# The order of eight running-maximum steps among the other VectorE work of a block, in the last stage of a four-layer kernel

## The chip, the cores and the metric

The kernel runs on one core of a Trainium2 chip. A core has five engines with instruction queues of their own: TensorE (PE in the profile, with its weight loads as PEld), VectorE (DVE), ScalarE (ACT), GpSimd (POOL) and SyncE (SP), which here only issues transfers. Each works through its queue in order, and they wait for one another, or for a transfer, through semaphores. The metric is the device time of one execution in microseconds, taken as the median of several runs.

## What is computed

The input `x` has 8 images of 32 channels, 256 rows and 256 columns, in fp32. Four layers follow one another, each of the form `x = x + conv(groupnorm(x))`: a spectral convolution, a 5 by 5 convolution, a recurrence over the columns, and a layer of directional maxima. The change lies in the last one:

```python
def _L3_conv_ref(x, W, b):
    x1 = cummax(x, axis=2)                 # down the rows
    x2 = cummax(x, axis=2, reverse=True)   # up the rows
    x3, x4 = ...                           # along the columns: from the left, from the right
    x_con = jnp.concatenate((x, x1, x2, x3, x4), axis=1)
    return jnp.einsum('bchw,oc->bohw', x_con, W[:, :, 0, 0]) + b[None, :, None, None]
x = x + _L3_conv_ref(_gn(x), L3_conv_W, L3_conv_b)
```

So each output is a mix, by a 160 to 32 matrix, of the normalised input and its running maxima in four directions.

## The kernel before

The stages run one after the other: `forward_and_mix` and `inverse_and_conv` (first two layers), `recurrence` (third layer), `maxima_and_mix` (last layer, from line 898, the only function that the change touches). The recurrence goes through the columns from left to right and leaves in device memory its output (`x3d`) and the maximum from the left (`fwd`), each as 32 blocks of 8 columns.

`maxima_and_mix` takes these blocks from the right end to the left, `bi` from 31 to 0, since the maximum from the right is carried from block to block. The rows of an image are folded by four: row 4q + a is element q (of Q = 64) of slot a (of A = 4). A tile has 128 partitions (four images of 32 channels), slots, two halves `b2` of the batch, 8 columns and 64 elements. The normalisation's scale is folded into the weights (`wsc`) and its shift into a bias (`bres`), so the maxima are taken of the values as they are.

Inside the loop the order on each engine is the order of the program text: `tc.manual_schedule(engines=None)` keeps the order written by hand. Semaphores for results and for buffers that come free are put in automatically. A block has these parts:

- **Loads** (`load`, line 965): SyncE issues the transfers of the next block, 2048 KB of `x3d` into `xt` and 2048 KB of `fwd` into `fw` (line 969). Both have two buffers.
- **VectorE, fifteen instructions.** Eight steps of the maximum from the right, column 7 down to column 0 (lines 989 to 994): each takes the maximum of the column and the result to its right, so each needs the one in front of it; the first needs column 0 of the block before (`after`). They write `rev` (tile `rv`, two buffers). Then the maxima over the rows: pairs of slots (line 1002, into `xt[:, A:A+2]`), all four slots (1003, into `top`), a scan over the 64 elements downwards into `dq` and one upwards into `uq` (1005, 1006), and three instructions that go back from folded to single rows, into `m` (1007, 1008, 1009). `m`, `dq`, `uq` and `top` have one buffer each.
- **TensorE, the mix** (`mix`, line 1019, and 1031 to 1036): for each half and each of the five terms, 16 products of 32 by 32 weights with 512 columns, all summed in PSUM, in four banks of a half. Two halves of two blocks take all eight banks. An fp32 product shows as two records, so a block has 320. Terms 0 (`x`), 3 (`fws`) and 4 (`rvs`, the maxima from the right) are mixed first for both halves; then come, half by half, 1 (`downs`) and 2 (`ups`), which need `m`, `dq` and `uq`.
- **ScalarE**: after a half's last term, four activations add the bias and move the four banks into `ot` (line 1039, three buffers), and ScalarE's queue issues its transfer to `out` (line 1040, 1024 KB).

```python
                for t, src in ((0, x), (3, fws), (4, rvs)):
                    for b2 in range(2):
                        mix(b2, t, src, first=t == 0)
                for b2 in range(2):
                    mix(b2, 1, downs)
                    mix(b2, 2, ups, last=True)
```

Of the kernel before, what the change touches and what calls it, by code (L numbers as in the profile page):

```python
# [11 lines left out]
ALU = mybir.AluOpType  # L12
# [11 lines left out]
A = 4  # L24
# [873 lines left out]
def maxima_and_mix(tc, k, d, x3d, fwd, mv3, mean1, out):  # L898


    nc = tc.nc
    WB = 8
    NB = W // WB
    with ExitStack() as ctx:
        one = ctx.enter_context(tc.tile_pool(name="cc", bufs=1))
        blk = ctx.enter_context(tc.tile_pool(name="cb", bufs=2))
        op = ctx.enter_context(tc.tile_pool(name="co", bufs=3))
        ps = ctx.enter_context(tc.tile_pool(name="cp", bufs=2, space=PSUM))

        w3 = one.tile([P, 5, C], F32, name="w3")  # L910
        b3 = one.tile([P, 1], F32, name="b3")
        nc.gpsimd.dma_start(out=w3.rearrange("p t o -> p (t o)"), in_=d["w3T"])
        nc.gpsimd.dma_start(out=b3, in_=d["b3"])


        sta, _ = finish_stats(tc, one, ps, k, mv3, B, k.pair, "c", "o1", 2)
        st = one.tile([P, 2, 2], F32, name="st3")
        for i in range(4):
            q = slice(32 * i, 32 * i + 32)
            nc.vector.tensor_copy(st[q], sta[q, i::4, :])  # L920
        shift = one.tile([P, 2], F32, name="shift3")
        nc.vector.scalar_tensor_tensor(shift, st[:, :, 0], -1.0, st[:, :, 1], ALU.mult, ALU.mult)
        wsc = one.tile([P, 2, 5, C], F32, name="wsc")
        for b2 in range(2):
            nc.vector.tensor_scalar_mul(wsc[:, b2], w3, st[:, b2, 1:2])

            nc.vector.tensor_tensor(wsc[:, b2, 0], wsc[:, b2, 0], k.ident32, ALU.add)


        wsum = one.tile([P, A, C], F32, name="wsum")  # L930
        nc.vector.tensor_tensor(wsum[:, 0], w3[:, 0], w3[:, 1], ALU.add)
        for t in range(2, 5):
            nc.vector.tensor_tensor(wsum[:, 0], wsum[:, 0], w3[:, t], ALU.add)
        for j in range(1, A):
            nc.vector.tensor_copy(wsum[:, j], wsum[:, 0])
        sel = one.tile([P, 2, 4], F32, name="sel")
        nc.vector.memset(sel, 0.0)
        for i in range(4):
            q = slice(32 * i, 32 * i + 32)
            nc.vector.tensor_copy(sel[q, :, i], shift[q])  # L940
        bp = ps.tile([P, 2, 4], F32, name="bp", tag="o0")
        nc.tensor.matmul(
            bp.rearrange("p b i -> p (b i)"),
            lhsT=wsum.rearrange("p j o -> p (j o)"),
            rhs=sel.rearrange("p b i -> p (b i)"),
            start=True,
            stop=True,
        )
        bres = one.tile([P, 2, 4], F32, name="bres")
        nc.vector.tensor_scalar_add(bres, bp, b3[:, 0:1])  # L950
        nc.vector.tensor_tensor(bres, bres, mean1.rearrange("p (b i) -> p b i", b=2), ALU.add)


        QP = Q + 2
        cuts = one.tile([P, 2, 2 * WB, QP], F32, name="cuts")
        nc.vector.memset(cuts, BIG)
        nc.vector.memset(cuts[:, 0, :, 0:1], -BIG)
        nc.vector.memset(cuts[:, 1, :, QP - 1 : QP], -BIG)
        cutf = cuts.rearrange("p s w q -> p s (w q)")
        top = one.tile([P, 2, WB, QP], F32, name="top")  # L960
        nc.vector.memset(top, -BIG)

        xs = {}

        def load(bi):

            for src, tag, n in ((x3d, "x3", A + 2), (fwd, "fw", A)):
                t = xs[bi, tag] = blk.tile([P, n, 2, WB, Q], F32, name=f"{tag}_{bi}", tag=tag)
                nc.sync.dma_start(out=t[:, 0:A].rearrange("p a b w q -> p (a b) (w q)"), in_=src[bi].rearrange("p a b n -> p (a b) n"))

        def flat(t):
            return t.rearrange("p s b w q -> p s (b w q)")

        def rows_of(t):
            return t.rearrange("p s b w q -> p s (b w) q")

        def twice(t):
            return t.rearrange("p b w q -> p (b w) q").unsqueeze(1).to_broadcast([P, 2, 2 * WB, Q])

        after = None  # L980
        with tc.manual_schedule(engines=None):
            load(NB - 1)
            for bi in range(NB - 1, -1, -1):
                if bi > 0:
                    load(bi - 1)
                xt, fw = xs.pop((bi, "x3")), xs.pop((bi, "fw"))
                rev = blk.tile([P, A, 2, WB, Q], F32, name=f"rv_{bi}", tag="rv")
                if after is not None:
                    nc.vector.tensor_tensor(rev[:, :, :, WB - 1, :], after, xt[:, 0:A, :, WB - 1, :], ALU.max)
                else:  # L990
                    nc.vector.tensor_copy(rev[:, :, :, WB - 1, :], xt[:, 0:A, :, WB - 1, :])
                for w in range(WB - 2, -1, -1):
                    nc.vector.tensor_tensor(rev[:, :, :, w, :], rev[:, :, :, w + 1, :], xt[:, 0:A, :, w, :], ALU.max)  # L993
                after = rev[:, :, :, 0, :]

                x = [xt[:, a] for a in range(A)]

                m = blk.tile([P, 6, 2, WB, Q], F32, name=f"m_{bi}", tag="m", bufs=1)
                dq = blk.tile([P, 2, WB, QP], F32, name=f"dq_{bi}", tag="dq", bufs=1)
                uq = blk.tile([P, 2, WB, QP], F32, name=f"uq_{bi}", tag="uq", bufs=1)  # L1000
                tt = nc.vector.tensor_tensor
                tt(flat(xt[:, A : A + 2]), flat(xt[:, 0:A:2]), flat(xt[:, 1:A:2]), ALU.max)  # L1002
                tt(top[:, :, :, 1 : 1 + Q], xt[:, A], xt[:, A + 1], ALU.max)
                df, uf, tf = (t.rearrange("p b w q -> p (b w q)") for t in (dq, uq, top))
                nc.vector.tensor_tensor_scan(df, cutf[:, 0], tf, -BIG, ALU.min, ALU.max)  # L1005
                nc.vector.tensor_tensor_scan(uf[:, ::-1], cutf[:, 1, ::-1], tf[:, ::-1], -BIG, ALU.min, ALU.max)
                tt(rows_of(m[:, 2:4]), twice(dq[:, :, :, 0:Q]), rows_of(xt[:, 0 : A + 1 : A]), ALU.max)  # L1007
                tt(rows_of(m[:, 0:2]), twice(uq[:, :, :, 2 : 2 + Q]), rows_of(xt[:, A - 1 : A + 2 : 2]), ALU.max)  # L1008
                tt(flat(m[:, 4:6]), flat(m[:, 1:4:2]), flat(xt[:, 1:3]), ALU.max)  # L1009
                downs = [m[:, 2], m[:, 3], m[:, 5], dq[:, :, :, 1 : 1 + Q]]  # L1010
                ups = [uq[:, :, :, 1 : 1 + Q], m[:, 4], m[:, 1], m[:, 0]]

                fws, rvs = [fw[:, a] for a in range(A)], [rev[:, a] for a in range(A)]
                pts = [
                    [ps.tile([P, 2 * H], F32, name=f"o_{bi}_{b2}_{i}", tag=f"o{i}") for i in range(4)] for b2 in range(2)
                ]


                def mix(b2, t, src, first=False, last=False):
                    for j in range(A):  # L1020
                        for i in range(4):
                            q = slice(32 * i, 32 * i + 32)
                            nc.tensor.matmul(  # L1023
                                pts[b2][i][32 * j : 32 * j + 32].rearrange("p (w q) -> p w q", q=Q),
                                lhsT=wsc[q, b2, t, :],
                                rhs=src[j][q, b2],
                                start=first,
                                stop=last,
                            )

                for t, src in ((0, x), (3, fws), (4, rvs)):
                    for b2 in range(2):
                        mix(b2, t, src, first=t == 0)
                for b2 in range(2):
                    mix(b2, 1, downs)
                    mix(b2, 2, ups, last=True)
                    ot = op.tile([P, 4, 2 * H], F32, name=f"ot_{bi}_{b2}", tag="ot")
                    for i in range(4):
                        nc.scalar.activation(ot[:, i], pts[b2][i], AF.Identity, bias=bres[:, b2, i : i + 1])  # L1039
                    nc.scalar.dma_start(out=out[bi, b2], in_=ot)  # L1040
# [140 lines left out]
```

## Time and profile before

| what | value |
|---|---|
| median of three runs | 3231.57 us (3227.11, 3231.57, 3237.39) |
| span of the profiled execution, first to last instruction | 3226.3 us |
| time of the profiled execution apart from its span | not given; the span is 0.8 us below the fastest of the three runs |
| busy over the span | PE 89%, DVE 81%, ACT 58%, POOL 27% |
| last stage, first load issued to the end of the span | 2545.7 to 3226.3 us, 680.6 us |
| DVE busy from 2600 to 3100 us, per 100 us | 97.9 to 98.1 us |
| PE busy in the same stretches | 75.9 to 78.6 us |
| moved by the transfers in the same stretches | 305 to 316 GB/s |

How to read what follows: rows of the profile name the line, engine, operation, output tile and input tiles, shapes (partitions times elements) and a count. In an answer in order of time the first number is the start in us from the span's start, the second the time from there to the end of the row; a bracket at its end gives the idle time of the engine before it and what ended it. Rows with the same line that stand in sequence are merged into one with a count. In the slices of the page each digit is a fortieth of the span, in tenths. In the table by stretches the columns are: the stretch, its length, the busy time of PE, PEld, DVE, ACT and POOL with instruction counts, the granted clock of TensorE as a share of full speed, the transfer engines' busy share, and GB/s.

### The profile page before, as it was taken

How to read it: one execution, taken by the hardware profiler on the slowest of the kernel's cores; microseconds unless marked ns; L12 is line 12 of the kernel's file. 1: busy time of each engine (PE TensorE's matmuls, PEld its weight loads, DVE VectorE, ACT ScalarE, POOL GpSimd, SP SyncE). 2: the span in 40 equal slices, each digit the busy share in tenths (PEclk: the TensorE clock that was granted, in tenths of full speed). 3: DMA queues.
4: the chain of work that ended last, by engine and by line, in shares of the span. 5: the costliest groups of instructions: out<-in, count | busy, mean ns of one | idle time of the engine just before them, and what ended most of it. 6: DMA issues, size and time to landing. Idle time of an engine off the chain costs nothing.

```text
span 3226.3 us, 112014 instructions
## 1 busy us (share of the span) xinstructions
PE 2866.3 (89%) x47802; PEld 1666.4 (52%) x47802; DVE 2614.3 (81%) x5188; ACT 1862.5 (58%) x4362; POOL 860.8 (27%) x1241
## 2 busy tenths in 40 slices
PE   7975799999999969999999999999999577777776
PEld 4655344444444446666666666666666233333332
DVE  5742577777767759999999999999999799999998
ACT  3422365565565657888888888888887222222222
POOL 0110011111111145555555555555555200000000
PEclk9985899999999989999999999999999788888998
DMA  9978577888777545665555555666554588878885
GB/s 385 387 288 193 129 187 193 196 194 195 186 182 197 138 110 153 159 159 151 146 148 147 147 146 151 157 159 159 155 143 121 188 306 305 308 311 314 313 308 217
DMA packets 527058, 655.75 MB, mean 203 GB/s; under 512 B 388825, under 2 KB 389737, under 8 KB 500829
## 3 DMA queue, kind: packets, MB, share of 16 engines
q1 hardware_dynamic: 483628, 494.33, 53.9%
q0 software_dynamic: 17200, 85.05, 8.1%
q10 hardware_dynamic: 25728, 69.21, 5.4%
q8 instruction: 374, 6.13, 0.8%
q14 instruction: 128, 1.04, 0.1%
HBM read 371.63 MB, written 272.63 MB: 200 GB/s over the span
## 4 chain that ended last, share of the span: by engine, by line
PE 54%; DVE 25%; DMA 8%; SPq 6%; issue 5%; ACT 2%; POOL 0%; DVEq 0%; ACTq 0%; POOLq 0%
PE r L742 13%; PE z L742 12%; PE ni L742 6%; PE nh L742 6%; DMA x2d<-x 6%; SPq L547 5%; DVE rv L993 5%; PE vp L490 4%; DVE x L527 3%; PE yp L131 3%; DVE dq L1005 2%; DVE m L1009 2%; DVE m L1007 2%; DVE x L1002 2%; DVE m L1008 2%
## 5 line engine op out<-in xcount | busy, mean ns | idle before, releaser
L750 PE MATMUL z<-hs,weights 64*64 64x256 f32 x4080 | 539.4, 382 | 0.0
L750 PE MATMUL r<-hs,weights 64*64 64x256 f32 x4080 | 525.2, 375 | 0.0
L750 PE MATMUL ni<-hs,weights 64*64 64x256 f32 x4080 | 524.9, 375 | 0.0
L832 POOL TENSOR_TENSOR xw<-xw,hs 128x256 f32<-128x256 f32 x496 | 339.5, 684 | 635.6 <-DVE hs L831 635.6
L527 DVE SCALAR_TENSOR_TENSOR x<-vp,r,x 64x512 f32<-64x512 f32 (+2 forms) x640 | 350.8, 563 | 164.6 <-PE vp L490 137.8
L1039 ACT ACTIVATE ot<-o,bres 128x512 f32<-128x512 f32 x256 | 155.4, 690 | 541.5 <-PE o L1023 533.9
L490 PE MATMUL vp<-x,c_conv 64*64 64x384 f32 (+2 forms) x4608 | 457.5, 514 | 0.2
L826 POOL TENSOR_TENSOR a<-zm,xn 128x256 f32<-128x256 f32 x510 | 372.7, 731 | 6.4 <-issue 6.2
L1023 PE MATMUL o<-m,wsc 32*32 32x512 f32 x3072 | 237.1, 830 | 152.9 <-DVE m L1009 106.3
L824 ACT ACTIVATE n<-n,bih 128x256 f32<-128x256 f32 x510 | 260.8, 511 | 184.4 <-DVE n L823 184.4
L490 PEld LDWEIGHTS vp<-x,c_conv 64*64 64x64 f32 x4608 | 238.3, 138 | 234.5 <-issue 128.5
L742 PE MATMUL z<-xn,weights 64*64 64x256 f32 x2040 | 305.3, 376 | 24.2 <-ACT xn L722 24.2
L742 PE MATMUL r<-hs,weights 64*64 64x256 f32 x2040 | 319.0, 389 | 4.4 <-DVE hs L831 3.4
L742 PE MATMUL r<-xn,weights 64*64 64x256 f32 x2040 | 305.6, 376 | 1.0 <-ACT rs L817 1.0
L742 PE MATMUL nh<-xn,weights 64*64 64x256 f32 x2040 | 305.7, 376 | 0.0
L742 PE MATMUL z<-hs,weights 64*64 64x256 f32 x2040 | 305.2, 376 | 0.0
L742 PE MATMUL ni<-hs,weights 64*64 64x256 f32 x2040 | 305.2, 375 | 0.0
L722 ACT ACTIVATE xn<-xw,shift,turned 128x256 f32<-128x256 f32 x496 | 291.9, 589 | 0.0
L750 PEld LDWEIGHTS ni<-hs,weights 64*64 64x64 f32 x4080 | 284.4, 133 | 0.3
L818 DVE SCALAR_TENSOR_TENSOR n<-nh,bhh,rs 128x256 f32<-128x256 f32 x510 | 246.3, 483 | 45.3 <-ACT rs L817 30.7
L750 PEld LDWEIGHTS r<-hs,weights 64*64 64x64 f32 x4080 | 281.1, 131 | 0.2
L817 ACT ACTIVATE rs<-r,brz 128x256 f32<-128x256 f32 x510 | 242.7, 476 | 50.8 <-PE r L750 30.3
(165 smaller groups left out, 6267.2 us busy)
## 6 DMA issues: line engine op xcount, KB each, us to landing
xb<-in_xl_dram POOLq DMA_DIRECT2D x96, 768.0 KB, 6.4
xa<-in_xt_dram SPq DMA_DIRECT2D x64, 1024.0 KB
x<-x3d SPq DMA_DIRECT2D x32, 2048.0 KB
fw<-fwd SPq DMA_DIRECT2D x32, 2048.0 KB
out_dram<-ot ACTq DMA_DIRECT2D x64, 1024.0 KB
xw<-x2d SPq DMA_DIRECT2D x31, 2048.0 KB
fwd<-fm SPq DMA_DIRECT2D x248, 256.0 KB
x3d<-xw SPq DMA_DIRECT2D x248, 256.0 KB
```

The costliest lines, as they stand in the source:

```text
L490: ins = nc.tensor.matmul(vps[bank][to], lhsT=k.conv[r, P : P + 64] if kind == 2 else k.conv[r, o], rhs=pair_of(u, ch, g, lo, hi, (2, 0)[i] ...
L527: nc.vector.scalar_tensor_tensor(x, src[o], r1[rows, g : g + 1], x, ALU.mult, ALU.add, accum_out=s1[rows, 0, n, ch, g : g + 1])
L547: (nc.gpsimd if 2 * u + ch == 2 * n - 1 and p % 2 else nc.sync).dma_start(out=x2d[b, a, c0 : c0 + CH, TS * t + lo : TS * t + hi].rearrange ...
L722: nc.scalar.activation(norms[bi][:, b, w], raws[bi][:, b, w], AF.Identity, bias=shift[:, b : b + 1], scale=sc[:, 1, b : b + 1])
L742: ins = nc.tensor.matmul(out[r], lhsT=weights[r, kind, gate, :], rhs=src[r], start=start, stop=stop)
L750: ins = nc.tensor.matmul(out[pairs[1 - i]], lhsT=weights[r, kind, gate, :], rhs=prev[r, :, q0 : q0 + Q], start=False, stop=stop,)
L817: rs = nc.scalar.activation(r, p["r"], AF.Sigmoid, bias=brz[:, 0:1])
L818: nc.vector.scalar_tensor_tensor(m, p["nh"], bhh[:, 2:3], r, ALU.add, ALU.mult)
L824: nc.scalar.activation(m, m, AF.Tanh, bias=bih[:, 2:3])
L826: product = nc.gpsimd.tensor_tensor(a, zm, cur, ALU.mult)
L832: nc.gpsimd.tensor_tensor(raw, raw, new, ALU.add)
L1023: nc.tensor.matmul(pts[b2][i][32 * j : 32 * j + 32].rearrange("p (w q) -> p w q", q=Q), lhsT=wsc[q, b2, t, :], rhs=src[j][q, b2], start=first,
```

## The change

The eight steps become a function `back(w)`, and its calls stand between the other VectorE instructions of the block: step 7 behind the pair maxima, then one step behind each following instruction, and steps 1 and 0 both behind the last. On TensorE the maxima from the right, term 4, go from third to last: `x`, `fws`, `downs` and `ups` are mixed for both halves, and then each half gets its `rvs` and is emptied. Number, operations and shapes of the instructions and the buffers stay as they are.

```diff
                 rev = blk.tile([P, A, 2, WB, Q], F32, name=f"rv_{bi}", tag="rv")
-                if after is not None:
-                    nc.vector.tensor_tensor(rev[:, :, :, WB - 1, :], after, xt[:, 0:A, :, WB - 1, :], ALU.max)
-                else:
-                    nc.vector.tensor_copy(rev[:, :, :, WB - 1, :], xt[:, 0:A, :, WB - 1, :])
-                for w in range(WB - 2, -1, -1):
-                    nc.vector.tensor_tensor(rev[:, :, :, w, :], rev[:, :, :, w + 1, :], xt[:, 0:A, :, w, :], ALU.max)
-                after = rev[:, :, :, 0, :]
...
+                def back(w):
+                    last = after if w == WB - 1 else rev[:, :, :, w + 1, :]
+                    if last is None:
+                        nc.vector.tensor_copy(rev[:, :, :, w, :], xt[:, 0:A, :, w, :])
+                    else:
+                        tt(rev[:, :, :, w, :], last, xt[:, 0:A, :, w, :], ALU.max)
+
                 tt(flat(xt[:, A : A + 2]), flat(xt[:, 0:A:2]), flat(xt[:, 1:A:2]), ALU.max)
+                back(7)
                 tt(top[:, :, :, 1 : 1 + Q], xt[:, A], xt[:, A + 1], ALU.max)
+                back(6)
                 nc.vector.tensor_tensor_scan(df, cutf[:, 0], tf, -BIG, ALU.min, ALU.max)
+                back(5)
                 nc.vector.tensor_tensor_scan(uf[:, ::-1], cutf[:, 1, ::-1], tf[:, ::-1], -BIG, ALU.min, ALU.max)
+                back(4)
                 tt(rows_of(m[:, 2:4]), twice(dq[:, :, :, 0:Q]), rows_of(xt[:, 0 : A + 1 : A]), ALU.max)
+                back(3)
                 tt(rows_of(m[:, 0:2]), twice(uq[:, :, :, 2 : 2 + Q]), rows_of(xt[:, A - 1 : A + 2 : 2]), ALU.max)
+                back(2)
                 tt(flat(m[:, 4:6]), flat(m[:, 1:4:2]), flat(xt[:, 1:3]), ALU.max)
+                back(1)
+                back(0)
+                after = rev[:, :, :, 0, :]
...
-                for t, src in ((0, x), (3, fws), (4, rvs)):
+                for t, src in ((0, x), (3, fws), (1, downs), (2, ups)):
                     for b2 in range(2):
                         mix(b2, t, src, first=t == 0)
                 for b2 in range(2):
-                    mix(b2, 1, downs)
-                    mix(b2, 2, ups, last=True)
+                    mix(b2, 4, rvs, last=True)
                     ot = op.tile([P, 4, 2 * H], F32, name=f"ot_{bi}_{b2}", tag="ot")
```

More of the change, by code (lines that the diff above doesn't have):

```diff
@@ L1001, in maxima_and_mix @@
                 tt = nc.vector.tensor_tensor
+                df, uf, tf = (t.rearrange("p b w q -> p (b w q)") for t in (dq, uq, top))
+                def back(w):
[4 more added lines that the diff above has]
+                        tt(rev[:, :, :, w, :], last, xt[:, 0:A, :, w, :], ALU.max)
                 tt(flat(xt[:, A : A + 2]), flat(xt[:, 0:A:2]), flat(xt[:, 1:A:2]), ALU.max)
+                back(7)
                 tt(top[:, :, :, 1 : 1 + Q], xt[:, A], xt[:, A + 1], ALU.max)
-                df, uf, tf = (t.rearrange("p b w q -> p (b w q)") for t in (dq, uq, top))
+                back(6)
                 nc.vector.tensor_tensor_scan(df, cutf[:, 0], tf, -BIG, ALU.min, ALU.max)
+                back(5)
                 nc.vector.tensor_tensor_scan(uf[:, ::-1], cutf[:, 1, ::-1], tf[:, ::-1], -BIG, ALU.min, ALU.max)
+                back(4)
                 tt(rows_of(m[:, 2:4]), twice(dq[:, :, :, 0:Q]), rows_of(xt[:, 0 : A + 1 : A]), ALU.max)
+                back(3)
                 tt(rows_of(m[:, 0:2]), twice(uq[:, :, :, 2 : 2 + Q]), rows_of(xt[:, A - 1 : A + 2 : 2]), ALU.max)
+                back(2)
                 tt(flat(m[:, 4:6]), flat(m[:, 1:4:2]), flat(xt[:, 1:3]), ALU.max)
+                back(1)
+                back(0)
+                after = rev[:, :, :, 0, :]
                 downs = [m[:, 2], m[:, 3], m[:, 5], dq[:, :, :, 1 : 1 + Q]]
```

## The prediction

> **What bounds the kernel now.** I read the page's slices first, to find the stage that the change touches, then VectorE's instructions in order of time for one block of that stage, then TensorE's and ScalarE's for the same block, then granted clocks by stretch, and last the end of the chain of waits.
>
> The slices (80.7 us each): the last stage is the last eight or nine digits.
>
> ```profile
> PE   7975799999999969999999999999999577777776
> DVE  5742577777767759999999999999999799999998
> ```
>
> From slice 32 on DVE is at 9 and PE at 7. In the stage VectorE is nearly always busy, TensorE is not. One block of it on VectorE (columns: start us, us, engine, line, operation, tiles, count):
>
> ```profile
> 2859.94 2.29 DVE L1009 TENSOR_TENSOR m<-m,x 128x2048 f32<-128x2048 f32 x1
> 2862.15 0.68 DVE L989 TENSOR_TENSOR rv<-rv,x 128x512 f32<-128x512 f32 x1
> 2862.87 5.05 DVE L993 TENSOR_TENSOR rv<-rv,x 128x512 f32<-128x512 f32 x7
> 2867.84 2.28 DVE L1002 TENSOR_TENSOR x<-x 128x2048 f32<-128x2048 f32 x1
> 2870.16 1.23 DVE L1003 TENSOR_TENSOR top<-x 128x1024 f32<-128x1024 f32 x1
> 2871.49 2.36 DVE L1005 TENSOR_TENSOR_SCAN dq<-cuts,top 128x1056 f32<-128x1056 f32 x1
> 2873.76 2.33 DVE L1006 TENSOR_TENSOR_SCAN uq<-cuts,top 128x1056 f32<-128x1056 f32 x1
> 2876.01 2.27 DVE L1007 TENSOR_TENSOR m<-dq,x 128x2048 f32<-128x2048 f32 x1
> 2878.19 2.28 DVE L1008 TENSOR_TENSOR m<-uq,x 128x2048 f32<-128x2048 f32 x1
> 2880.51 2.29 DVE L1009 TENSOR_TENSOR m<-m,x 128x2048 f32<-128x2048 f32 x1
> 2882.72 0.68 DVE L989 TENSOR_TENSOR rv<-rv,x 128x512 f32<-128x512 f32 x1
> ```
>
> L989 recurs after 2882.72 - 2862.15 = 20.57 us, the period of all middle blocks; 32 blocks make 658 us. No wait for another engine stands in this list. What differs is where an instruction starts against the end of the one before it. One that doesn't need its forerunner's result starts before that one's recorded end: L1007 at 2876.01, L1006 ends at 2873.76 + 2.33 = 2876.09, so 0.08 early (L989, L1002, L1006 and L1008 likewise, 0.08 to 0.09). One that does need it starts late: L1003 by 2870.16 - 2870.12 = 0.04, L1009 by 0.04, L1005 by 0.10, L993 by about 0.03. Ten of the fifteen instructions are of this kind: seven L993, L1003, L1005, L1009.
>
> TensorE and ScalarE in the same block:
>
> ```profile
> 2862.29 0.63 PE L1023 MATMUL o<-m,wsc 32*32 32x512 f32 x4 [3.12 <-DVE m L1009]
> 2873.74 2.68 PE L1023 MATMUL o<-rv,wsc 32*32 32x512 f32 x60
> 2878.33 1.09 PE L1023 MATMUL o<-m,wsc 32*32 32x512 f32 x16 [1.90 <-DVE m L1007]
> 2882.86 1.08 PE L1023 MATMUL o<-m,wsc 32*32 32x512 f32 x4 [3.44 <-DVE m L1009]
> ```
>
> ```profile
> 2865.58 2.43 ACT L1039 ACTIVATE ot<-o,bres 128x512 f32<-128x512 f32 x4 [14.59 <-PE o L1023]
> 2868.48 2.43 ACT L1039 ACTIVATE ot<-o,bres 128x512 f32<-128x512 f32 x4 [0.47 <-PE o L1023]
> ```
>
> TensorE has idled 1.90 + 3.44 = 5.3 us by the end of a block, waiting for VectorE: that is its slack. Its clock over a block:
>
> ```profile
> 2882.80:2886.00 3.20, 3.14 (x64) 1.21 (x65) 3.06 (x6) 0.00 (x0) 0.00 (x0) 0.50 0.68 205
> 2886.00:2890.00 4.00, 4.00 (x102) 1.89 (x79) 3.90 (x5) 2.73 (x5) 0.00 (x0) 0.89 1.01 430
> 2890.00:2899.00 9.00, 7.72 (x176) 3.47 (x166) 8.86 (x6) 2.12 (x4) 0.00 (x0) 1.00 0.98 377
> ```
>
> The third number from the right is the granted clock: half for some 4 us after the idle time, then full. And the end of the program:
>
> ```profile
> 3211.92 7.03 PE o L1023 x112
> 3218.95 2.41 ACT ot L1039 x4
> ```
>
> **What the Trainium skill says.** "Perfetto Trace Analysis", section "DVE / Act Engine Instruction (TENSOR_ADD, Activation, etc)": the recorded span ends with the write's acknowledgement, the next instruction may begin to fetch before that, and the semaphore is seen only after it. The trace agrees: 0.08 us early without a dependency, 0.03 to 0.10 late with one. "VectorE: DVE Perf Modes", section "The DRAIN you can't avoid", reports that a semaphore behind each operation cost nothing extra in a test of copies; the rows above differ by some 0.12 us, and I go by them. "TensorE: Matmul & The Clock Gate", section "What's actually happening": the array's clock falls to half after an idle window and rises after about 3.4 us of work; the clock column agrees (0.50, 0.89, 1.00).
>
> **The change, VectorE's part.** The fifteen instructions remain, with their shapes; only the order changes: L1002, step 7, L1003, step 6, scan, step 5, scan, step 4, L1007, step 3, L1008, step 2, L1009, steps 1 and 0. A needed result is now two places back, with one exception (step 0 behind step 1). What becomes of each stall, from start-to-start times:
> - Steps: a dependent one takes (5.05 - 0.69) / 6 = 0.727 us, an independent one 0.69 - 0.085 = 0.607 (the sum checks: six of 0.727 and one of 0.607 give 4.97 = 2867.84 - 2862.87). Seven stalls become one: 6 x 0.12 = 0.72 us.
> - L1002 to L1003: 2.32 becomes 2.20 (as L1006 to L1007: duration less 0.085). 0.12 us.
> - L1003 to L1005: 1.33 becomes 1.14. 0.19 us.
> - L1008 to L1009: 2.32 becomes 2.20. 0.12 us.
>
> Sum 1.15 us a block, period 19.42. That a result two places back is free is seen at L1007, which needs L1005 and starts 0.08 early behind L1006; that it holds behind a step of 0.6 us, not 2.3, is an inference: the stall to be covered is 0.12 to 0.19 us. Bounds for the cover: full (taken), or only the three behind long operations, 0.43 us a block. I see no reason for a loss in VectorE itself. 32 x 1.15 = 36.6 us.
>
> **TensorE's part.** 320 matmul records a block, as before. The x and fw mixes stay first. The mixes of downs and ups for both halves now come together, the steps' mix behind them. I count from R, the end of L1009, the release of 112 of the 128 records of downs and ups (the x16 row needs only L1007).
> - 112 records: 7.03 us at half clock (the row at the end), some 4.4 at full. I take the worse.
> - Steps' mix: 64 records take 2.23 us at full clock (fw's first start to rv's first start, 2871.06 to 2873.29). Step 0 ends 1.3 us after R, long before TensorE asks for it. The first half is complete at R + 8.4.
> - ScalarE empties its four banks in 2.43 us, then 0.47, then the second half in 2.43: done at R + 13.7. All eight PSUM banks are in use, so the next block's x mix waits for this. Before, the first half was complete 3.3 us after R (2865.58) and its emptying lay beside the second half's mixes; now 1.1 us of work covers it. This is the one thing that gets worse in the middle of the stage.
> - The last x mixes and fw (64 records): fw ended about 2.4 + 0.3 us behind the emptying, hence R + 16.5; the 16 records that need L1007: R + 17.6. The next R is at R + 19.4.
>
> So TensorE has 1.8 us left where it had 3.4 in front of L1009, and the bound stays on VectorE. Does it hold VectorE through the single buffers? From R, in half clock: dq is read by R + 3.1 (48 records), rewritten at R + 1.3 + 4.5 = R + 5.8; uq read by R + 5.6, rewritten at R + 8.7; m read by R + 7.0, rewritten at R + 11.6. No wait. rv has two buffers and over 10 us to spare.
>
> **Transfers.** SP's two loads (x, fw) still go out when the last reader of the block is done: before L1009 (2862.30), now step 0, at the same place in the period. Output goes out from R + 10.8 instead of R + 5.9. A block moves 6.3 MB: 306 GB/s at 20.57 us, 324 at 19.42, and the transfer view of this block shows stretches of 437. The DVE waits for a load once in the stage, at its first block (12.3 us), which stays. Cost nothing; should it not be hidden, a late load would show as a DMA wait in front of L1002.
>
> **The end.** Before: R, 7.03, then 2.41, then the store. Now: 112 + 32 records, R + 8.1 to 9.1 (clock), then 2.43 + 0.47 + 2.43: R + 13.9, against R + 9.5; but R lies 1.3 us before VectorE's end. +3.1 us (bounds 0, at full clock, and +3.6).
>
> **Sum.** 3226.3 - 36.6 + 3.1 = 3192.8 us for the profiled execution. Its span is 5.3 below the median of the runs; I subtract the same 33.5 from the median: **3198**.
>
> **Rivals.**
> - Half cover: only the long operations' stalls go. 32 x 0.43 - 3 = 11: 3221. For it, no row shows a short step between two dependent ones; against it, the stall is a fifth of a step's length. Chance 0.04.
> - The change does nothing for VectorE, the stall belonging to the form and not to the dependency; only the tail stays: 3235. Against it, L1002 and L1009 have one form and start 0.08 early and 0.04 late. Chance 0.03.
> - **Slower:** TensorE takes over. With half clock for the whole block: emptying 5.3, end of the x mix 1.0, fw 64 x 0.07 = 4.5, 128 records of downs and ups 8.0, first half of the steps' mix 2.2: 21.0 us a block, through the PSUM banks. 32 x 0.45 + 3 = 17: 3249. It decides where TensorE's cycle passes 19.4 us, that is, where half clock lasts past the steps' mix and through fw. For it: in the last blocks half clock lasts up to 7 us, and emptying is exposed. Against it: in the middle blocks the clock is full after 4 to 5 us of work. Chance 0.08.
>
> **Chances and range.** The forecast has 0.85. Its own range: steps of 0.684 us (as L989) and no longer tail would give 40 less than now, and the runs scatter by 5: 3188; a longer tail, TensorE late in some blocks and the scatter give 3213. Outside lie the rivals with 0.15 and little else, so that is the range. About 0.3% (9.7 us) is what a measurement of this kernel can tell from no change: faster 0.88 (the forecast and most of the half cover), same 0.04, slower 0.08.
>
> **What would show it.** VectorE's period 19.4 us in place of 20.57; L1003, L1009 and both scans starting 0.08 early; only step 0 late. TensorE's wait for L1009 shrunk from 3.4 to 1 to 3 us and the wait for L1007 gone; ScalarE starting 7 to 9 us after L1009. Wrong, if VectorE shows waits for PE at a scan or L1007, or if TensorE no longer idles.

## The result, and the profile after

| | before | after |
|---|---|---|
| median of four runs each | 3229.34 us | 3196.34 us |
| span of the profiled execution | 3226.3 us | 3193.9 us |
| its time apart from the span | not given | 3195.71 us |
| VectorE's part of the stage, first to last instruction | 2553.98 to 3211.86: 657.9 us | 2558.01 to 3178.04: 620.0 us |
| from there to the end of the span | 14.4 us | 15.9 us |
| DVE / PE busy, DVE period | 98 / 76%, 20.57 us | 99.8 / 83%, 19.38 us |

The ratio of the times is 0.9892 (95% interval 0.9875 to 0.9910): 1.1% faster. (The busy shares are those of 2650 to 3150 us.) The two spans differ by 32.4 us: VectorE's part gives 37.9, the end takes back 1.4, and everything in front of the stage happened to take 4.0 longer in the profiled execution of after, which no part of the change touches.

The slices of the page, in the same order as before:

```profile
PE   7985799999989969999999999999999678888887
DVE  5752577777767748999999999999999799999997
```

VectorE is at 9 again; TensorE has gone from 7 to 8, mostly since the same work now has less time around it. One block on VectorE in order of time (start, length, engine, line, operation, tiles). The line numbers from here on are those of the kernel after, where not said otherwise: steps L1001, pair maxima L1003, `top` L1005, the scans L1007 (`dq`) and L1009 (`uq`), and the three maxima into `m` L1011, L1013 and L1015 (L1007, L1008 and L1009 before).

```profile
2867.85 2.29 DVE L1003 TENSOR_TENSOR x<-x 128x2048 f32<-128x2048 f32 x1
2870.05 0.68 DVE L1001 TENSOR_TENSOR rv<-rv,x 128x512 f32<-128x512 f32 x1
2870.66 1.22 DVE L1005 TENSOR_TENSOR top<-x 128x1024 f32<-128x1024 f32 x1
2871.79 0.68 DVE L1001 TENSOR_TENSOR rv<-rv,x 128x512 f32<-128x512 f32 x1
2872.39 2.35 DVE L1007 TENSOR_TENSOR_SCAN dq<-cuts,top 128x1056 f32<-128x1056 f32 x1
2874.66 0.67 DVE L1001 TENSOR_TENSOR rv<-rv,x 128x512 f32<-128x512 f32 x1
2875.25 2.35 DVE L1009 TENSOR_TENSOR_SCAN uq<-cuts,top 128x1056 f32<-128x1056 f32 x1
...
2883.70 2.28 DVE L1015 TENSOR_TENSOR m<-m,x 128x2048 f32<-128x2048 f32 x1
2885.91 1.41 DVE L1001 TENSOR_TENSOR rv<-rv,x 128x512 f32<-128x512 f32 x2
2887.23 2.28 DVE L1003 TENSOR_TENSOR x<-x 128x2048 f32<-128x2048 f32 x1
```

Recorded lengths are nearly those of before (a step 0.67 to 0.69 us, a scan 2.35). What has changed is where the next one starts: after a step at 2870.05 + 0.68 = 2870.73, L1005 starts at 2870.66; the scan starts 0.08 before the end of the step in front of it, where it used to start 0.10 behind the end of `top`. Only steps 1 and 0, which stand as a pair behind L1015, still hold a stall: 1.41 - 0.68 = 0.73 from one start to the next, against 0.60 for a step elsewhere (2870.05 + 0.61 = 2870.66).

TensorE and ScalarE behind the L1015 of this block, a few rows of each:

```profile
2886.04 0.63 PE L1032 MATMUL o<-m,wsc 32*32 32x512 f32 x4 [2.79 <-DVE m L1015]
2887.88 1.15 PE L1032 MATMUL o<-dq,wsc 32*32 32x512 f32 x4
2890.95 0.64 PE L1032 MATMUL o<-rv,wsc 32*32 32x512 f32 x2
2893.70 5.33 PE L1032 MATMUL o<-x,wsc 32*32 32x512 f32 x51
2898.89 2.37 PE L1032 MATMUL o<-fw,wsc 32*32 32x512 f32 x49
```

```profile
2892.97 2.42 ACT L1047 ACTIVATE ot<-o,bres 128x512 f32<-128x512 f32 x4 [14.04 <-PE o L1032]
2895.86 2.42 ACT L1047 ACTIVATE ot<-o,bres 128x512 f32<-128x512 f32 x4 [0.47 <-ACT ot L1047]
```

Of TensorE's two waits in a block one is left, here 2.79 us in front of the last maximum (L1015). One block is no measure of it, since it goes from 1.7 to 4.4 us over the stage. The wait lists have the sums (total in us, times, longest), first of before and then of after:

```profile
PE o L1023 <- DVE m L1009: 106.3, 32, 3.4
PE o L1023 <- DVE m L1007: 46.6, 30, 6.5
```

```profile
PE o L1032 <- DVE m L1015: 104.0, 32, 4.4
PE o L1032 <- DVE m L1011: 5.2, 1, 5.2
```

So the wait for the last maximum has stayed what it was, 3.3 us a block on average, and the one for the first maximum into `m` has gone. The 112 records behind L1015 take 2890.95 - 2886.04 = 4.9 us to issue. ScalarE begins 7.0 us after the end of L1015 (2885.98), where it began 3.3 us after; the two halves follow each other at its own speed. The next `x` mix goes at ScalarE's pace (51 records in 5.33 us, where 49 of `fw` take 2.37; weight loads wait 126.5 us for ScalarE over the stage), since the two halves of a single block hold all eight PSUM banks, not those of two blocks.

### The profile page after: what moved, and what is told of

It is laid out like the page before. It is cut to its first block, busy times and chain, and to the rows that moved or that the text cites. A ratio compares the mean times of both kernels' runs of the same rounds, so it can differ in the third digit from the quotient of the medians.

```text
span 3193.9 us, 112013 instructions
## 1 busy us (share of the span) xinstructions
PE 2870.8 (90%) x47802; PEld 1672.7 (52%) x47802; DVE 2589.1 (81%) x5188; ACT 1856.4 (58%) x4362; POOL 862.3 (27%) x1241
## 4 chain that ended last, share of the span: by engine, by line
PE 60%; DVE 24%; DMA 5%; issue 4%; SPq 4%; ACT 2%; POOL 0%; DVEq 0%; ACTq 0%; POOLq 0%
PE r L742 13%; PE z L742 12%; PE vp L490 8%; PE ni L742 6%; PE nh L742 6%; DVE x L527 4%; DVE rv L1001 4%; PE up L424 4%; SPq L547 3%; PE yp L131 2%; DVE dq L1007 2%; DMA x2d<-x 2%; DVE uq L1009 2%; DVE m L1015 2%; DVE m L1013 2%
## 5 line engine op out<-in xcount | busy, mean ns | idle before, releaser
L1032 PE MATMUL o<-m,wsc 32*32 32x512 f32 x3072 | 226.0, 716 | 110.8 <-DVE m L1015 104.0
```

Of the source, the lines that this page charges most:

```text
L1032: nc.tensor.matmul(pts[b2][i][32 * j : 32 * j + 32].rearrange("p (w q) -> p w q", q=Q), lhsT=wsc[q, b2, t, :], rhs=src[j][q, b2], start=first,
```

## The experiments

The theory: VectorE sets the period, and the gain is the time that an instruction loses when it needs the result of the one right in front of it. Rivals: the gain comes from the new order on TensorE; or the stall belongs to short instructions in a row, whatever they need; or TensorE has become the bound. Each run is compared with runs of the kernel before on the same chip (medians 3224.8 to 3226.9 us), so ratios can be set side by side, and times of different runs only roughly. Edits are shown against the kernel after; those of "TensorE's new order alone" and of "Both old orders, steps that need nothing" are shown against the kernel before.

### The steps alone, with TensorE's old order

```diff
-                for t, src in ((0, x), (3, fws), (1, downs), (2, ups)):
+                for t, src in ((0, x), (3, fws), (4, rvs)):
...
-                    mix(b2, 4, rvs, last=True)
+                    mix(b2, 1, downs)
+                    mix(b2, 2, ups, last=True)
```

> VectorE's new order with TensorE's old one: the steps' mix third, downs and ups half by half. Theory: the new place of the mix is needed, because TensorE now stands at the steps' mix until step 0 ends (1.3 us after L1009's counterpart) and reads dq for the second half only 160 records later, some 7.7 us, while the next scan wants to overwrite dq 5.8 us after that release. VectorE stalls at the scan for about 3 us a block, the period is near 22.6 us and the time about 3290 (3230 if TensorE's clock is full throughout). Rival: only VectorE's order counts and TensorE has slack enough: 3196, as with the whole change.

Measured: 3299.22 us, ratio 1.0221 (1.0202 to 1.0241): 2.2% slower than before. VectorE and TensorE of this kernel in order of time:

```profile
2873.17 0.68 DVE L1001 TENSOR_TENSOR rv<-rv,x 128x512 f32<-128x512 f32 x1
2877.26 2.36 DVE L1007 TENSOR_TENSOR_SCAN dq<-cuts,top 128x1056 f32<-128x1056 f32 x1 [3.41 <-PE o L1032]
```

```profile
2869.37 4.09 PE L1032 MATMUL o<-rv,wsc 32*32 32x512 f32 x64 [7.44 <-DVE rv L1001]
```

TensorE stands 7.44 us at the steps' mix until step 0 is done, although x and fw are mixed and `m` is waiting; then the reading of `dq` for the second half comes too late for the next scan, which waits 3.41 us. The wait list has 101.4 us for that scan over 31 blocks. VectorE's part of the stage is 724.2 us. Half of the change, the half that removes the stalls, loses more than the whole gains.

### The steps alone, with two buffers for dq and uq

On top of the edit of the run before:

```diff
-                dq = blk.tile([P, 2, WB, QP], F32, name=f"dq_{bi}", tag="dq", bufs=1)
-                uq = blk.tile([P, 2, WB, QP], F32, name=f"uq_{bi}", tag="uq", bufs=1)
+                dq = blk.tile([P, 2, WB, QP], F32, name=f"dq_{bi}", tag="dq", bufs=2)
+                uq = blk.tile([P, 2, WB, QP], F32, name=f"uq_{bi}", tag="uq", bufs=2)
```

> The steps alone (VectorE's new order, TensorE's old one) with two buffers in place of one for dq and uq. Theory: the 3.4 us of stall at the scan are the single buffer of dq and nothing else; with two the period returns to 19.4 us, though TensorE still waits for step 0: 3196 to 3202. Rival: TensorE's late start at step 0 is itself the bound, and the wait moves to the next shared tile (m): above 3250.

Measured: 3195.90 us, ratio 0.9906 (0.9890 to 0.9923). No wait for PE on VectorE, its part of the stage 620.0 us as with the change. TensorE still idles for step 0:

```profile
PE o L1032 <- DVE rv L1001: 140.1, 32, 12.4
```

So the loss of the run before was the single buffers. The late start of TensorE costs VectorE nothing by itself; only the end is longer, 17.1 us behind VectorE's last instruction, where it is 15.9 with the change. The run also shows what the second half of the change is worth: TensorE's new order does with one buffer each what otherwise takes two.

### TensorE's new order alone

```diff
-                for t, src in ((0, x), (3, fws), (4, rvs)):
+                for t, src in ((0, x), (3, fws), (1, downs), (2, ups)):
...
-                    mix(b2, 1, downs)
-                    mix(b2, 2, ups, last=True)
+                    mix(b2, 4, rvs, last=True)
```

> The old order on VectorE with the steps' mix last on TensorE. Theory: the gain is all VectorE's, so the period stays 20.57 us, and only the longer end shows: 3229 + 3 = 3232. Rival: the regrouping on TensorE brings some of the gain: below 3220.

Measured: 3229.05 us, ratio 1.0006 (0.9997 to 1.0014). VectorE's part is 657.9 us to the tenth of before. The end grew: ScalarE's last row starts 9.9 us after the end of VectorE's last instruction (3221.62 against 3209.46 + 2.29), where before it started 7.1 us after (3218.93 against 3211.86). The rival that TensorE's order brings some of the gain falls.

### Both old orders, steps that need nothing

```diff
-                    nc.vector.tensor_tensor(rev[:, :, :, WB - 1, :], after, xt[:, 0:A, :, WB - 1, :], ALU.max)
+                    nc.vector.tensor_tensor(rev[:, :, :, WB - 1, :], xt[:, 0:A, :, 0, :], xt[:, 0:A, :, WB - 1, :], ALU.max)
...
-                    nc.vector.tensor_tensor(rev[:, :, :, w, :], rev[:, :, :, w + 1, :], xt[:, 0:A, :, w, :], ALU.max)
+                    nc.vector.tensor_tensor(rev[:, :, :, w, :], xt[:, 0:A, :, w + 1, :], xt[:, 0:A, :, w, :], ALU.max)
```

> Both old orders, but each step takes the maximum of two columns of the input in place of a column and the result to its right, so no step needs the one in front (the carried maximum from the right is left out; same number and shapes of instructions). Theory: the stall comes of the dependency, so seven stalls of 0.12 us go without any reordering: the period falls by 0.84 to 19.73, 27 us less than before: 3202. Rival: the stall belongs to short instructions in a row: no change, 3229.

Measured: 3195.81 us, ratio 0.9908 (0.9891 to 0.9925). The steps on VectorE, in a row as before the change:

```profile
2867.17 0.68 DVE L989 TENSOR_TENSOR rv<-x 128x512 f32<-128x512 f32 x1
2867.77 4.30 DVE L993 TENSOR_TENSOR rv<-x 128x512 f32<-128x512 f32 x7
2871.99 2.28 DVE L1002 TENSOR_TENSOR x<-x 128x2048 f32<-128x2048 f32 x1
```

(4.30 - 0.69) / 6 = 0.60 us from step to step, where the same row of before has 5.05 and 0.727. Nothing is reordered and the shapes are the same; only the need of the forerunner's result is gone. VectorE's part is 630.2 us, 27.7 less than before: 0.87 a block, or 0.124 for each of seven steps. That is the dependency, and not the length or the neighbourhood of a step. The whole change gains 10.2 us more on VectorE, from the three long operations' stalls less the one pair of steps that stays (0.20 + 0.12 + 0.12 - 0.12 = 0.32 a block, 10.2 in all). These 10.2 us rest on the traces alone. The times don't resolve them (31 us less than before here, 33.0 and 34.2 with the change): the end gives 2.0 of them back (13.9 us here, 15.9 with the change), and what stands in front of the stage, the same in all these kernels, scatters, with VectorE's part starting anywhere between 2550.7 and 2560.2 us in these profiles.

### The mix half by half

```diff
-                for t, src in ((0, x), (3, fws), (1, downs), (2, ups)):
+                for t, src in ((0, x), (3, fws)):
...
                 for b2 in range(2):
+                    mix(b2, 1, downs)
+                    mix(b2, 2, ups)
                     mix(b2, 4, rvs, last=True)
```

> The whole change, but after x and fw the mix runs half by half: downs, ups and steps of the first half, its emptying, then those of the second. Theory: emptying of the first half is covered again, but dq is now read to the end only 112 records after L1009's counterpart, about 5.5 to 7 us, and the next scan wants it after 5.8 us: VectorE stalls for 0 to 1.2 us a block: 3196 to 3233, likeliest 3210. Rival: the covered emptying is worth more than that and the time falls below 3193.

Measured: 3221.96 us, ratio 0.9988 (0.9981 to 0.9995). That is 4.9 us less than before, where the change gains 33.0 and 34.2, so some 28 us of the gain are lost. The time is in the range expected, and the stall near its upper end:

```profile
2882.94 2.36 DVE L1007 TENSOR_TENSOR_SCAN dq<-cuts,top 128x1056 f32<-128x1056 f32 x1 [1.01 <-PE o L1032]
```

1.01 us in a block, 31.6 in all, at the same scan for the same buffer; VectorE's part is 654.4 us. ScalarE's emptying is covered again here, which shortens the end by 1.0 us (14.8 in place of 15.9) and gains nothing in the middle. Most of a 1% gain hangs on reading `dq` for both halves before anything else.

### The steps further ahead

The order on VectorE is `back(7)`, L1003, `back(6)`, L1005, `back(5)`, scan, `back(4)`, scan, `back(3)`, `back(2)`, L1011, `back(1)`, L1013, `back(0)`, L1015 by the lines of after; on TensorE:

```diff
-                for t, src in ((0, x), (3, fws), (1, downs), (2, ups)):
+                for t, src in ((0, x), (3, fws), (4, rvs), (1, downs)):
...
-                    mix(b2, 4, rvs, last=True)
+                    mix(b2, 2, ups, last=True)
```

> Another order of the same instructions: step 7, L1003, step 6, L1005, step 5, scan, step 4, scan, step 3, step 2, L1011, step 1, L1013, step 0, L1015, and on TensorE x, fw, steps, downs for both halves, then ups half by half. Theory: one adjacent pair is left as in the change (3 and 2), so VectorE's period is again 19.4; step 0 ends 2.2 us before L1015, dq is read 128 records later, some 6.7 us from there, 0.6 us before the next scan wants it: 3196, as the change. Rival: the margin at dq fails and VectorE stalls there: above 3205.

Measured: 3190.65 us, ratio 0.9895 (0.9880 to 0.9910), VectorE's part 620.0 us. The change itself on the same chip:

> The change itself once more, on the same chip as the three others, for comparison with them: 3196, ratio to before 0.989 to 0.991.

Measured: 3190.89 us, ratio 0.9896 (0.9881 to 0.9911). The two can't be told apart. The particular order is not what counts: fifteen instructions with one adjacent pair left take 620.0 us in either, as long as `dq` is read in time.

### More work for TensorE

```diff
-                for t, src in ((0, x), (3, fws), (1, downs), (2, ups)):
+                for t, src in ((0, x), (3, fws), (3, fws), (1, downs), (2, ups)):
```

> The whole change with the mix of the maxima from the left (fw) done twice, so that its term counts double in the output: 64 more matmul records a block, 2.2 us at full clock. Theory: after the change TensorE still idles 2.8 us in front of L1015, so the added work fits and the time stays at that of the change, 3196 (within 3). Rival: TensorE is already at the bound, and each block grows by 2.2 us: 3265.

Measured: 3192.02 us, ratio 0.9899 (0.9884 to 0.9914); VectorE's part 620.0 us. As expected, if it is held against the change on the same chip (3190.89) and not against 3196. TensorE's waits in front of L1015 are down from 104.0 to 18.6 us over the stage. The next run, with `(3, fws)` three times in that line, was to put TensorE over the edge:

> The whole change with the fw mix done three times (its term counts three times in the output): 128 more records than the change, 4.5 us at full clock. Theory: TensorE's slack in front of L1015 is 2.8 us, of which the doubled mix left 0.6; now TensorE sets the period, 19.4 - 0.6 + 2.2 = 21.0 us, and VectorE waits for PE at a tile with one buffer: 3192 + 52 = 3244. Rival: the pause of 1.4 us without a releaser that TensorE showed in the doubled run is slack too, so only 0.2 us a block is missing: 3200.

Measured: 3192.45 us, ratio 0.9898 (0.9882 to 0.9915): the theory's 3244 is wrong. The rival's 3200 is nearer, but its reason doesn't reach: more than a wait and a pause has been used up. Clock and busy time by stretch, over most of the stage (columns as in the table of before; third from the right is the granted clock), for the change, the doubled and the tripled mix:

```profile
2650.00:3150.00 500.00, 412.67 (x8264) 179.06 (x8268) 499.10 (x389) 126.01 (x208) 0.00 (x0) 0.94 0.85 327
```

```profile
2650.00:3150.00 500.00, 455.81 (x9926) 207.93 (x9930) 499.10 (x388) 126.02 (x208) 0.00 (x0) 0.98 0.86 327
```

```profile
2650.00:3150.00 500.00, 463.33 (x11411) 239.49 (x11398) 490.02 (x381) 121.01 (x200) 0.00 (x0) 0.99 0.81 319
```

The records per block went up by 20 and by 40%, the busy time by 10 and 12%. Two things made room. First the waits: for L1011 and L1015 TensorE waits 109.2 us over the stage of the change and 4.1 in the tripled run. Then the records themselves: in one block of the tripled run all 128 of `downs` and `ups` are issued in 4.2 us (first of them 2868.67, first of `rv` 2872.90), where in the change 112 took 4.9. The granted clock goes with the idle time, from 0.94 to 0.99; in the other direction, the run with the steps alone, in which TensorE waits 242.6 us for step 0, has 0.80 over the same stretch.

The profiled execution of the tripled run is the longest of its four (3203.31; the others 3192.15 to 3192.49). In it TensorE waits for L1015 only once, VectorE's two scans wait 9.0 us for PE, where the change has no such wait, and VectorE's part is 630.3 us. So the margin was used up there; the other three executions are as fast as the change, and how much further one could go wasn't tried.

## Why the prediction was right, step by step

- **VectorE as the bound, and the stall as the thing removed:** right. Predicted period 19.42 us, measured 19.38; sum 36.6 (32 x 1.15 is 36.8, a slip), measured 37.9. A step took 0.604 from start to start, not 0.607, and steps two back from their forerunner record 0.68 in place of 0.69. That a short step covers the stall was inferred; the rows of after show it at every step, and the free steps show that the dependency is the cause. The Trainium skill, "Vector Engine (DVE) Microarchitecture Reference", section "5.2 Measured stream behaviour on trn2", gives, for back-to-back instructions on mostly 32-bit integers, one element a cycle at 0.96 GHz plus about 75 ns per instruction after queue overlap. An estimate from it for a step is 512 / 0.96 + 75 = 608 ns, and the trace has 604. In this trace that is the price of a step that needs nothing from the instruction right in front; a needed result adds 0.12 us.
- **No wait for the single buffers:** right, and with the times listed: `dq` was to be read by R + 3.1 and rewritten at R + 5.8, and in the block above its last reading ends at 2887.88 + 1.15 = 2889.03, 3.05 us after the end of L1015, while the next L1007 starts at 2891.77, 5.8 after. This margin belongs to the order of the mixes: the mix half by half, one small step away, loses 1.01 us a block at `dq`.
- **TensorE's slack:** the size was wrong. The prediction put 7.03 us on the 112 records, at half clock, and had 1.8 us left in front of L1015, with a wait of 1 to 3 us to show for it; the records took 4.9 in the block above, and the wait stayed at 3.3 on average. The runs with more work show that even this is no limit: 128 more records, 4.5 us at full clock, went in. The rival with half clock for the whole block takes the clock as fixed while TensorE works without a pause; in the tripled run, which comes closest to that, the granted clock was 0.99. It fell where TensorE idled: 0.70 from 2886.0 to 2889.4, right behind the wait in the block above, and 1.00 from 2893 on.
- **The end:** +3.1 predicted, 1.4 measured, from the same term: ScalarE's first row of the last block starts 6.9 us after L1015's end instead of 8.1 to 9.1.
- **The total** of -33.5 against -33.0 between the medians is closer than its terms, and in that by luck: VectorE gave 1.3 more than predicted and the end took 1.7 less, while the part in front of the stage was 4.0 longer in the profiled execution. Such a scatter is what the range allowed for.
- **Transfers:** right. 327 GB/s were moved instead of 307, and VectorE's only wait for a load is that of the first block (12.3 us, in front of L1003).

## What to carry to other kernels

Where one engine is busy to the last tenth, look at the starts and not only at the lengths: an instruction that starts behind the recorded end of its forerunner is losing time to it, and an independent one put between takes that time back (here 37.9 us on VectorE, for 1.4 at the end). Before moving work in this way, follow the tiles that have one buffer: who reads them last on the other engine, and whether that reading still comes before the next writing; the reordering here is worth 1% with the readings put first and costs 2% without. And don't take TensorE's idle time for its slack: here, work that filled the idle time also brought the clock back.

## What the runs showed of the hardware

- On VectorE a needed result from the instruction right in front costs 0.12 us in these maxima (0.727 against 0.604 us from start to start) and 0.20 in front of a scan (1.33 against 1.13). One independent instruction of 0.6 us between hides either: each then starts 0.08 us before the recorded end of the one in front.
- TensorE took in 40% more matmul records in a block of hardly changed length (19.4 us with 20% more, 630.3 / 32 = 19.7 in the profiled execution with 40% more), while its mean granted clock from 2650 to 3150 us went from 0.94 to 0.98 and 0.99.
